# Node rows and kept sums moved in quarters, and VectorE's side tasks dealt anew over eight batches

## The chip, the core and the metric

The kernel runs on one core of one Trainium2 chip. The core has TensorE (PE in the profile), VectorE (DVE), ScalarE (ACT), GpSimd (POOL) and SyncE (SP), which each follow their own instruction stream and wait for one another by semaphores. SP and POOL issue the transfers: SP plain copies between HBM and the on-chip memory SBUF, POOL the gathers (indirect transfers that read rows by a list of indices). 16 DMA engines carry them. TensorE writes to PSUM, eight banks of 2 KB in each of 128 partitions.

The metric is the device time of one execution in microseconds.

## The reference

A graph network's block (PaiNN) on 1250 nodes of 512 numbers and 40,000 edges, sorted by their target node, and then a layer norm of the sum of input and block:

```python
x_j = x[src]
v_j = x_j[:, :384].reshape(E, 128, 3)
s_j = silu(x_j[:, 384:] @ W1 + b1) @ W3 + b3
rbf = sqrt(2 / R_CUT) * sin(n * pi * r / R_CUT) / r          # n = 1..20
cutoff = 0.5 * (cos(pi * r / R_CUT) + 1.0) * (r < R_CUT)
split = s_j * (rbf * cutoff @ W2 + b2)
s1, s2, s3 = split[:, :128], split[:, 128:256], split[:, 256:]
v_msg = v_j * s1[:, :, None] + s3[:, :, None] * edge_attr1[:, None, :]
x = x + segment_sum(concat([v_msg.reshape(E, 384), s2]), dst)
x_j = x[src]
v = x_j[:, :384].reshape(E, 3, 128) @ U
v_V = v @ V
norm = linalg.norm(v_V.reshape(E, 128, 3), axis=2)
h = silu(concat([norm, x_j[:, 384:]]) @ Wu1 + bu1) @ Wu2 + bu2
v = v * h[:, :128, None]
scal = einsum('ijk,ijk->ij', v, v_V) + h[:, 256:]
x = x + segment_sum(concat([v.reshape(E, 384), scal]), dst)
out = layernorm(x0 + x)
```

## The kernel before, in words

The first half of the block depends on an edge only through its source row and its distance. So a table with one row of 640 numbers (2560 bytes) for each node is written to HBM first (`table1`, about the first 25 us). Then the main loop in `windowed` runs over the 40,000 edges in 80 batches, `t` = 0 to 79. A batch has four tiles of 128 edges (the last four batches have fewer), one from each of four neighbouring chunks of 512 sorted edges; four batches make a group, two groups a block of 128 nodes, so a block's edges are done every eight batches. Block `b` "begins" at batch 8b + 8, when its sums are complete.

One batch does this:

- `gather(t + 4)`: POOL issues four indirect transfers (line 746) that fetch the table rows of a batch four batches ahead, into one of five buffers ("rooms", named `more` and `nodes` in the profile). The first of the four waits for `made`, the last matrix product of the factors of the next batch.
- `edge_factors(t + 1)` (line 882): PE computes from the radial basis the factors `eb` of the next batch, in four PSUM banks that exist once. So it waits until VectorE has read the factors of the present batch, and VectorE's next batch waits for it.
- `messages(t)`: VectorE makes the one-hot rows `hot` (L841), two products of the gathered rows with the factors (L893, which waits for the rows, and L896, the last reader of `eb`), `spread` (L851) and the pair of marks `pair` (L911).
- `add_messages(t - 1)` and `count_links(t - 1)`: PE adds the messages by node and counts the edges by source and target, with one-hot rows that ScalarE makes (L863, L873).

Beside the batches runs the work on finished blocks, which a plan deals to the batches by hand. `at(when, step, rank, fn, ...)` puts a task into one of the lists `first`, `early`, `late` and `dve`; in each batch the loop at line 1550 issues `messages`, `first`, the sums and counts, `early`, the factors, the gather, `late` and `dve`, each list in order of rank. An engine carries out what it is given in this order. VectorE's own tasks stand in `dve`, after L911, where PE is busy with the next factors.

For block `b`, with steps counted from its begin, the tasks that matter here are: `sum_block` (PE sums the block in the single PSUM bank `work`, steps 0 and 1), `fetch_nodes` (SP loads the block's 128 rows of x into `node_x`, 256 KB, step -3), `take_block` (VectorE adds both: L1032 for 384 columns, L1037 for 128, step 1), `turn_nodes` (step 3), `keep_rest` (L1042, step 4: VectorE writes x + x1 into the buffer `h_t`, and SP stores it as `resid`, 256 KB), then the second half's products by node, `scale_row` (L1166, step 8), `dot_row` (L1175, step 9), `end_row` (PE, step 10, list `early`, in a `work` bank: L1144, L1145, L1098), and `part_row`, which splits the row into an upper (ScalarE) and a lower part (VectorE, L1205, step 13).

`work()` gives out one PSUM bank; each call takes it anew, for another purpose. The second segment sum is a product of the matrix of edge counts with these split rows: `begin_out` does parts of it ahead, from batch 32 on, in slots of the plan (`ready` says from which batch a unit may run), and stores ("spills", L1297) each started sum through SP, 256 KB. The rest follows after the loop, with the layer norm.

`make_turns` prepares the arguments of the sine for two groups at a time on VectorE: part 0 multiplies (L769), part 1 rounds (L775), part 2 subtracts (L782, twice), part 3 is ScalarE's sine.

Of the kernel before, what the change touches and what calls it, by code (L numbers as in the profile page):

```python
# [11 lines left out]
F32 = mybir.dt.float32  # L12
# [5 lines left out]
ALU = mybir.AluOpType  # L18
# [3 lines left out]
P = 128  # L22
C = 128
V = 3 * C
R_CUT = 1.4415
N_RBF = 20
EPS = 1e-05
MAGIC = 12582912.0
# [562 lines left out]
def windowed(tc, sh):  # L591
# [63 lines left out]
    with tc.tile_pool(name="msg", bufs=4) as pool, tc.tile_pool(  # L655
# [84 lines left out]
        def gather(t, behind=None):  # L740

            g, i = batches[t]
            rows_t = next(rooms)
            for j in tiles(g, i):
                n = lanes(g, i, j)
                got = nc.gpsimd.indirect_dma_start(  # L746
                    out=rows_t[:n, j, :],
                    out_offset=None,
                    in_=sh.table1,
                    in_offset=bass.IndirectOffsetOnAxis(  # L750
                        ap=sh.src_i[:n, g, i * CPG + j : i * CPG + j + 1], axis=0
                    ),
                )
                if behind is not None and j == 0:
                    tc.add_manual_dep(
                        got.ins, behind.ins.name, sync,
                        reason="so that rows come while PE is ahead of DVE",
                    )
            clear_rest(t, rows_t, nc.gpsimd)
            rows_of[t] = rows_t  # L760


        def make_turns(g, n, part):

            shape = [P, n, EPG, N_RBF]
            args = turn[:, :n].rearrange("p g t n -> p (g t n)")
            if part == 0:
                share = ratio[:, g * EPG : (g + n) * EPG].rearrange("p (g t) -> p g t", t=EPG)
                nc.vector.tensor_mul(  # L769
                    turn[:, :n], share[:, :, :, None].to_broadcast(shape),  # L770
                    halves[-1][:, None, None, :].to_broadcast(shape),
                )
            elif part == 1:
                wholes[g] = rbf.tile([P, 2 * N_RBF * EPG], F32, name="whole")[:, : n * N_RBF * EPG]
                nc.vector.tensor_scalar(  # L775
                    wholes[g], args, MAGIC, MAGIC, op0=ALU.add, op1=ALU.subtract
                )
            elif part == 2:
                whole = wholes.pop(g)
                for k in range(n):  # L780
                    cols = slice(k * N_RBF * EPG, (k + 1) * N_RBF * EPG)
                    nc.vector.tensor_sub(args[:, cols], args[:, cols], whole[:, cols])  # L782
            elif part == 3:
                nc.scalar.activation(args, args, AF.Sin, scale=TWO_PI)

        wholes = {}

        basis = sh.basis
        halves, fading = [sh.half_n], {0: fade[:, :EPG]}
# [231 lines left out]
        node_x = sh.node_x  # L1021

        def fetch_nodes(b):
            if b == NB - 1:
                rows = sh.n_nodes + MARGIN - b * P
                nc.gpsimd.memset(node_x[rows // 32 * 32 :, :], 0.0)
            load_nodes(nc.sync, sh, node_x[:, None, :], b, b + 1, slice(0, width), b)

        def take_block(b):
            blk, xb = blks.pop(b), node_x  # L1030
            x1 = pool.tile([P, width], F32, name="x1", bufs=2)
            nc.vector.tensor_add(  # L1032
                x1[:, :V].rearrange("p (c k) -> p k c", k=3),
                xb[:, :V].rearrange("p (c k) -> p k c", k=3),
                by_component(blk[:, :V]),
            )
            nc.vector.tensor_add(x1[:, V:], xb[:, V:], blk[:, V:])  # L1037
            x1s[b] = x1

        def keep_rest(b):  # L1040
            both = sh.h_t[:, :width]
            nc.vector.tensor_add(both, x1s[b], node_x)  # L1042
            if b == NB - 1:
                rest[b] = both
                return
            nc.sync.dma_start(resid[b * P : (b + 1) * P, :], both)


        upd = {}
# [293 lines left out]
            last_step[g] = t  # L1343


        first, early, late, dve = {}, {}, {}, {}

        def at(when, step, rank, fn, *args):
            when.setdefault(step, []).append((rank, fn, args))
# [26 lines left out]
        for b in range(NB):  # L1376
            begin = last_step[2 * b + 1] + 1
            begins.append(begin)
            if b < NB - 1:
                assert begin == 8 * b + 8  # L1380
                at(late, begin, 1, sum_block, b, 0)
                at(first, begin + 1, 1, sum_block, b, 1)
                links_at = (
                    (dve, 1, 1, take_block), (dve, 4, 3, keep_rest), (early, 3, 6, turn_nodes),
                    (early, 4, 1, times_u), (late, 4, 1, times_uv), (late, 5, 1, lengths),
                    (first, 6, 3, root), (late, 6, 1, hidden), (first, 7, 1, curve),
                    (late, 7, 1, factors), (dve, 8, 1, scale_row),
                    (dve, 9 if begin + 10 < NT else 8, 3, dot_row),
                )
# [12 lines left out]
            if b in by_vector:  # L1402
                for step in (4, 8) if b < NB - 1 else (2, 6):
                    if b < NB - 1 and step == 4:
                        at(first, begin + step + 1, 0, add_parts, b)
                    else:
                        at(dve, begin + step, 4, add_parts, b)
            at(dve, begin - 3, 9, fetch_nodes, b)
            for when, step, rank, fn in links_at:
                at(when, begin + step, rank, fn, b)  # L1410
            when, step, rank = last
            if begin + step < NT:
                ends[b] = end = begin + step
                at(when, end, rank, end_row, b)
                parts = (first, end + 1, 2), (dve, end + 3, 2)
            else:
                ends[b] = end = begin + min(step, 9)
                at(first, end, 1, end_row, b)
                parts = ((dve, end, 9),) * 2 if b < NB - 1 else ((dve, end - 1, 2),)
            if b == NB - 3:  # L1420
                parts = parts[0], (dve, NT - 1, 9)
            if b == NB - 2:
                parts = parts[0], (dve, begins[b] + 10, 5)
            for k, (when, step, rank) in enumerate(parts):
                at(when, step, rank, part_row, b, k)
# [16 lines left out]
        after = 0  # L1442
        free_slots = [(8 * c + step, when) for c in range(4, NB) for step, when in slots]
        for chain, a in units:
            ready = max(ends[a] + 4, last_step[2 * chain[0] + 1] + 4, after)
            while free_slots[0][0] < ready:
                free_slots.pop(0)
            step, when = free_slots.pop(0)
            if a == chain[1]:
                block = (a, chain[2], chain[0], 1)  # L1450
                at(dve, step - 1, 9, cast_counts, nc.scalar.copy, "cast", CASTS, NB - 1, [block])
            at(when, step, 8, begin_out, chain, a)
            after = step + 1 if a == chain[2] - 1 else step
# [93 lines left out]
        for t in range(min(ahead, NT)):  # L1547
            gather(t)
        edge_factors(0)
        for t in range(max(*first, *early, *late, *dve) + 1):  # L1550
            if t < NT:
                messages(t)
            run(first, t)
            if 1 <= t <= NT:
                add_messages(t - 1)
                count_links(t - 1)
            run(early, t)
            if t + 1 < NT:
                made = edge_factors(t + 1)
            if t + ahead < NT:  # L1560
                gather(t + ahead, made if t + ahead < NT - 2 else None)
            run(late, t)
            run(dve, t)
        assert NB == ACCS + 3
# [371 lines left out]
```

## Time and profile before

| | us |
|---|---|
| three runs | 479.78, 477.28, 478.63 |
| median | 478.63 |
| the profiled execution | 479.63 |
| its span, first to last instruction | 477.8 |
| VectorE busy | 421.4 |
| TensorE busy (mean granted clock 0.947) | 406.7 |
| ScalarE busy | 372.1 |
| GpSimd busy | 339.3 |

The profile is of one execution. A row of a timeline has the start, the duration, the engine, the line, the operation, what it writes and reads, and in brackets the engine's idle time just before it and what ended it. A row of a group of instructions has the line, the engine, the operation with its tiles, the count, then the busy time, the mean in ns, and the idle time before. "issue" as the end of an idle time means that nothing in the profile was waited for. Names of tiles are the program's own.

### The profile page before, as it was taken

The page shows a single profiled execution, that of the slowest core. Times are in us where ns is not written, and L with a number is a line of the kernel's source. Part 1 is how long each engine was busy: PE and PEld are TensorE (multiplying, and loading weights), DVE is VectorE, ACT ScalarE, POOL GpSimd, SP SyncE. Part 2 cuts the span into 40 slices and gives each one's busy share as a digit, 9 for nine tenths or more (in the row PEclk, how much of TensorE's full clock was granted, in tenths as well). Part 3 has the DMA queues.
Part 4 walks back from the last instruction along what each step waited for, and adds up shares of the span by engine and source line. Part 5 has one row for each costly group of instructions (what it writes and reads, how often), then busy time and mean ns, then how long its engine had stood idle before and what let it go on. Part 6 is the DMA issues. An engine that isn't in the chain of part 4 may idle for free.

```text
span 477.8 us, 11146 instructions
## 1 busy us (share of the span) xinstructions
PE 406.7 (85%) x4233; PEld 230.0 (48%) x4233; DVE 421.4 (88%) x666; ACT 372.1 (78%) x971; POOL 339.3 (71%) x366
## 2 busy tenths in 40 slices
PE   5847678888887887898899899988999989899993
PEld 3423343454444454455445545644554654455782
DVE  5889999888999998899999899998999898896693
ACT  3556877686989879579898899888999798586573
POOL 7367777777777777777777777777777777763940
PEclk9956989897999999799999999999999999899997
DMA  8898888898889889888998988888898898889123
GB/s 255 307 266 262 263 261 257 257 301 259 255 258 308 259 268 301 256 264 259 306 295 278 319 285 286 292 276 275 292 310 284 284 300 271 248 281 365 42 100 123
DMA packets 39107, 126.96 MB, mean 266 GB/s; under 512 B 6801, under 2 KB 9119, under 8 KB 39043
## 3 DMA queue, kind: packets, MB, share of 16 engines
q0 software_dynamic: 25824, 104.47, 69.5%
q1 hardware_dynamic: 11610, 20.56, 12.4%
q10 hardware_dynamic: 1608, 1.12, 0.8%
q8 instruction: 35, 0.57, 0.5%
q14 instruction: 30, 0.24, 0.1%
HBM read 114.78 MB, written 11.34 MB: 264 GB/s over the span
## 4 chain that ended last, share of the span: by engine, by line
PE 24%; DVE 22%; POOL 20%; DMA 16%; issue 13%; ACT 2%; DVEq 0%; ACTq 0%; POOLq 0%
POOL more L746 14%; DMA more<-table,src_i 10%; POOL nodes L746 6%; DVE more L896 6%; PE eb L882 6%; DMA nodes<-table,src_i 5%; DVE more L893 4%; PE agg L927 3%; DVE nodes L896 3%; DVE spread L851 2%; PE agg L933 2%; PE eb L1279 1%; PE adj L1279 1%; DVE nodes L893 1%; PE pp L311 1%
## 5 line engine op out<-in xcount | busy, mean ns | idle before, releaser
L746 POOL DMA_INDIRECT more<-table,src_i x189 | 182.7, 967 | 66.1 <-issue 48.3
L746 POOL DMA_INDIRECT nodes<-table,src_i x124 | 119.1, 960 | 37.8 <-issue 31.7
L873 ACT ACTIVATE one<-one,weight,src_f 128x128 f16<-128x128 f16 x313 | 128.5, 482 | 0.4 <-DVE src_f L723 0.2
L882 PE MATMUL eb<-w_sb,basis_t 25*128 25x388 f32 x626 | 79.2, 564 | 48.8 <-DVE more L896 29.8
L863 ACT ACTIVATE one<-number,low 128x128 f16<-128x128 f16 x313 | 99.7, 392 | 2.4 <-PE adj L956 2.4
L896 DVE TENSOR_TENSOR more<-more,eb 128x1536 f32<-128x1536 f32 (+2 forms) x49 | 82.8, 1691 | 0.0
L893 DVE TENSOR_TENSOR more<-more,eb 128x1024 f32<-128x1024 f32 (+2 forms) x49 | 57.7, 1178 | 8.2 <-issue 4.7
L882 PEld LDWEIGHTS eb<-w_sb,basis_t 25*128 25x128 f32 x626 | 26.5, 193 | 70.0 <-DVE more L896 41.8
L896 DVE TENSOR_TENSOR nodes<-nodes,eb 128x1536 f32<-128x1536 f32 (+1 forms) x32 | 54.3, 1697 | 0.0
L927 PE MATMUL agg<-more,hot 128*32 128x512 f32 x378 | 54.0, 636 | 0.0
L933 PEld LDWEIGHTS agg<-more,spread 128*32 128x32 f32 x1134 | 35.6, 116 | 31.1 <-issue 31.0
L851 DVE TENSOR_TENSOR spread<-hot,eb 128x384 f32<-128x384 f32 (+1 forms) x81 | 43.2, 534 | 0.0
L893 DVE TENSOR_TENSOR nodes<-nodes,eb 128x1024 f32<-128x1024 f32 (+1 forms) x32 | 37.9, 1183 | 5.8 <-DMA nodes<-table,src_i 5.2
L933 PE MATMUL agg<-more,spread 128*32 128x128 f32 x1134 | 42.9, 285 | 0.0
L911 DVE TENSOR_TENSOR pair<-number,column 128x640 f16<-128x640 f16 (+1 forms) x81 | 38.7, 479 | 0.0
L841 DVE TENSOR_TENSOR hot<-lane,eb 128x128 f32<-128x128 f32 (+1 forms) x81 | 22.6, 280 | 16.8 <-PE eb L882 16.6
L956 PE MATMUL adj<-pair,one 128*128 128x160 f16 x313 | 36.8, 241 | 0.0
L927 PE MATMUL agg<-nodes,hot 128*32 128x512 f32 x248 | 35.6, 630 | 0.0
L933 PEld LDWEIGHTS agg<-nodes,spread 128*32 128x32 f32 x744 | 22.8, 113 | 20.5 <-issue 20.4
L956 PEld LDWEIGHTS <-one 128*128 128x128 f16 x313 | 22.3, 102 | 13.1 <-issue 11.8
L933 PE MATMUL agg<-nodes,spread 128*32 128x128 f32 x744 | 27.5, 277 | 0.0
L824 ACT COPY basis_t<-work 128x512 f32<-128x512 f32 x20 | 11.7, 586 | 19.3 <-PE work L819 19.2
(268 smaller groups left out, 679.9 us busy)
## 6 DMA issues: line engine op xcount, KB each, us to landing
table<-more SPq DMA_DIRECT2D x10, 320.0 KB
spilled<-begun SPq DMA_DIRECT2D x12, 256.0 KB
more<-table,src_i POOLq DMA_INDIRECT x189
more<-spilled SPq DMA_DIRECT2D x2, 1280.0 KB
resid<-h_t SPq DMA_DIRECT2D x9, 256.0 KB
node_x<-in_x_dram SPq DMA_DIRECT2D x8, 256.0 KB
nodes<-table,src_i POOLq DMA_INDIRECT x124
nodes<-in_x_dram POOLq DMA_DIRECT2D x2, 768.0 KB
```

The lines of the kernel that those rows point to most:

```text
L746: got = nc.gpsimd.indirect_dma_start(out=rows_t[:n, j, :], out_offset=None, in_=sh.table1, in_offset=bass.IndirectOffsetOnAxis(ap=sh.src_i ...
L841: nc.vector.tensor_tensor(hots[t][:m, js, :], lane[:m, None, :WIN].to_broadcast(shape), eb[:m, js, V + 3 : V + 4].to_broadcast(shape), op= ...
L851: nc.vector.tensor_mul(spread[t][:m, js], hots[t][:m, js, None, :].to_broadcast(shape), eb[:m, js, V : V + 3, None].to_broadcast(shape),)
L863: nc.scalar.activation(onehots[t][:, j, :], number[:, :P], AF.Abs, bias=low[:, e : e + 1])
L873: nc.scalar.activation(one, one, AF.Relu, scale=less[:, e : e + 1], bias=worth[:, e : e + 1])
L882: made = nc.tensor.matmul(eb[:, j, : V + CARRY], turned[g][rows, i, :], sh.w2_sb[rows, :], start=True, stop=True,)
L893: nc.vector.tensor_mul(msg[:m, js, V:], msg[:m, js, V:], eb[:m, js, C:V])
L896: nc.vector.tensor_mul(msg[:m, js, :V].rearrange("p t (k c) -> p t k c", k=3), msg[:m, js, :V].rearrange("p t (k c) -> p t k c", k=3), eb[ ...
L911: nc.vector.tensor_tensor(pair[:m, js, :].rearrange("p t (l h) -> p t l h", h=2), number[:m, : PARTS * WIN].rearrange("p (l h) -> p l h", ...
L927: nc.tensor.matmul(agg[j * WIN : (j + 1) * WIN, :], hots[t][:, j, :], msg[:, j, :width], start=(i == 0), stop=False, skip_group_check=True,)
L933: nc.tensor.matmul(agg[j * WIN : (j + 1) * WIN, c * C : (c + 1) * C], spread[t][:, j, c, :], msg[:, j, width:], start=False, stop=(i == la ...
L956: nc.tensor.matmul(to[:, :, at : at + WIN], one[:m, j, :], pair[:m, j, :].rearrange("e (p n) -> e p n", n=WIN), start=(i == 0 and j == js[ ...
```

## The change

- `fetch_nodes` of blocks 0 to 8 becomes `fetch_part` in four batches, steps -3 to 0: 32 of 128 rows each, 64 KB. The store of `resid` leaves `keep_rest` and becomes `keep_part` in four batches, steps 8 to 11, for blocks 0 to 7. Both stand in a new list `mid`, which is issued after the gather and before `late`, and each transfer waits for `made`, PE's factors of the next batch. Blocks 8 and 9 keep whole transfers for what is left.
- `take_block` is split: `take_v` (L1032) stays at step 1, `take_s` (L1037) goes to step 2.
- The lower half of `part_row` (L1205) goes from step 13 to step 11. With it `ready` in the plan of the second sum goes from ends + 4 to ends + 2.
- Parts 1 and 2 of `make_turns` no longer round both groups and then subtract for both, but do both for one group each, with a rounding of 320 numbers instead of 640.

```diff
-            elif part == 1:
-                wholes[g] = rbf.tile([P, 2 * N_RBF * EPG], F32, name="whole")[:, : n * N_RBF * EPG]
-                nc.vector.tensor_scalar(
-                    wholes[g], args, MAGIC, MAGIC, op0=ALU.add, op1=ALU.subtract
-                )
-            elif part == 2:
-                whole = wholes.pop(g)
-                for k in range(n):
+            elif part in (1, 2):
+                for k in range(part - 1, min(part, n)):
                     cols = slice(k * N_RBF * EPG, (k + 1) * N_RBF * EPG)
-                    nc.vector.tensor_sub(args[:, cols], args[:, cols], whole[:, cols])
+                    whole = rbf.tile([P, N_RBF * EPG], F32, name="whole", bufs=2)
+                    nc.vector.tensor_scalar(
+                        whole, args[:, cols], MAGIC, MAGIC, op0=ALU.add, op1=ALU.subtract
+                    )
+                    nc.vector.tensor_sub(args[:, cols], args[:, cols], whole)
...
+        QUARTER = P // 4
+
+        def fetch_part(b, k):
+            low, high, node = places(sh, b)
+            first, end = max(low, k * QUARTER), min(high, (k + 1) * QUARTER)
+            at_node = node + first - low
+            for i, j in by_sixteen(end - first):
+                after_factors(nc.sync.dma_start(
+                    node_x[first + i : first + j, :], sh.x[at_node + i : at_node + j, :]
+                ))
+
+        def after_factors(got):
+            tc.add_manual_dep(
+                got.ins, made.ins.name, sync, reason="so that transfers spread over the batches"
+            )
+
+        def keep_part(b, k):
+            rows = slice(k * QUARTER, (k + 1) * QUARTER)
+            after_factors(nc.sync.dma_start(
+                resid[b * P + rows.start : b * P + rows.stop, :], sh.h_t[rows, :width]
+            ))
...
+        def take_s(b):
+            nc.vector.tensor_add(x1s[b][:, V:], node_x[:, V:], blks.pop(b)[:, V:])
...
             if b == NB - 1:
                 rest[b] = both
-                return
-            nc.sync.dma_start(resid[b * P : (b + 1) * P, :], both)
+            if b == NB - 2:
+                nc.sync.dma_start(resid[b * P : (b + 1) * P, :], both)
...
-                    (dve, 1, 1, take_block), (dve, 4, 3, keep_rest), (early, 3, 6, turn_nodes),
+                    (dve, 1, 1, take_v), (dve, 2, 1, take_s), (dve, 4, 3, keep_rest),
+                    (early, 3, 6, turn_nodes),
...
-            at(dve, begin - 3, 9, fetch_nodes, b)
+            if b < NB - 1:
+                for k in range(4):
+                    at(mid, begin - 3 + k, 1, fetch_part, b, k)
+            else:
+                at(dve, begin - 3, 9, fetch_nodes, b)
+            if b < NB - 2:
+                for k in range(4):
+                    at(mid, begin + 8 + k, 2, keep_part, b, k)
...
-                parts = (first, end + 1, 2), (dve, end + 3, 2)
+                parts = (first, end + 1, 2), (dve, end + 1, 6)
...
-            ready = max(ends[a] + 4, last_step[2 * chain[0] + 1] + 4, after)
+            ready = max(ends[a] + 2, last_step[2 * chain[0] + 1] + 4, after)
...
                 gather(t + ahead, made if t + ahead < NT - 2 else None)
+            run(mid, t)
             run(late, t)
             run(dve, t)
```

More of the change, by code (lines that the diff above doesn't have):

```diff
@@ L772, in make_turns @@
                 )
-            elif part == 1:
-                wholes[g] = rbf.tile([P, 2 * N_RBF * EPG], F32, name="whole")[:, : n * N_RBF * EPG]
-                nc.vector.tensor_scalar(
-                    wholes[g], args, MAGIC, MAGIC, op0=ALU.add, op1=ALU.subtract
-                )
-            elif part == 2:
-                whole = wholes.pop(g)
-                for k in range(n):
-                    cols = slice(k * N_RBF * EPG, (k + 1) * N_RBF * EPG)
-                    nc.vector.tensor_sub(args[:, cols], args[:, cols], whole[:, cols])
+            elif part in (1, 2):
+                for k in range(part - 1, min(part, n)):
+                    cols = slice(k * N_RBF * EPG, (k + 1) * N_RBF * EPG)
+                    whole = rbf.tile([P, N_RBF * EPG], F32, name="whole", bufs=2)
[3 more added lines that the diff above has]
+                    nc.vector.tensor_sub(args[:, cols], args[:, cols], whole)
             elif part == 3:
                 nc.scalar.activation(args, args, AF.Sin, scale=TWO_PI)
-        wholes = {}
         basis = sh.basis
@@ L1023, in fetch_nodes, with take_v @@
         def fetch_nodes(b):
-            if b == NB - 1:
-                rows = sh.n_nodes + MARGIN - b * P
-                nc.gpsimd.memset(node_x[rows // 32 * 32 :, :], 0.0)
+            rows = sh.n_nodes + MARGIN - b * P
+            nc.gpsimd.memset(node_x[rows // 32 * 32 :, :], 0.0)
             load_nodes(nc.sync, sh, node_x[:, None, :], b, b + 1, slice(0, width), b)
-        def take_block(b):
-            blk, xb = blks.pop(b), node_x
-            x1 = pool.tile([P, width], F32, name="x1", bufs=2)
+        QUARTER = P // 4
[16 more added lines that the diff above has]
+            ))
+        def take_block(b):
+            take_v(b)
+            take_s(b)
+        def take_v(b):
+            blk, xb = blks[b], node_x
+            x1s[b] = x1 = pool.tile([P, width], F32, name="x1", bufs=2)
             nc.vector.tensor_add(
@@ L1036, in take_block @@
             )
-            nc.vector.tensor_add(x1[:, V:], xb[:, V:], blk[:, V:])
-            x1s[b] = x1
+        def take_s(b):
+            nc.vector.tensor_add(x1s[b][:, V:], node_x[:, V:], blks.pop(b)[:, V:])
         def keep_rest(b):
@@ L1343, in windowed @@
             last_step[g] = t
-        first, early, late, dve = {}, {}, {}, {}
+        first, early, late, dve, mid = {}, {}, {}, {}, {}
         def at(when, step, rank, fn, *args):
@@ L1549, in windowed @@
         edge_factors(0)
-        for t in range(max(*first, *early, *late, *dve) + 1):
+        for t in range(max(*first, *early, *late, *dve, *mid) + 1):
             if t < NT:
```

## The prediction

> **What bounds the kernel now.** I read the page first: VectorE (DVE) is the busiest engine by its share, TensorE (PE) next, GpSimd (POOL) only fourth.
>
> ```profile
> span 477.8 us, 11146 instructions
> PE 406.7 (85%) x4233; PEld 230.0 (48%) x4233; DVE 421.4 (88%) x666; ACT 372.1 (78%) x971; POOL 339.3 (71%) x366
> ...
> L746 POOL DMA_INDIRECT more<-table,src_i x189 | 182.7, 967 | 66.1 <-issue 48.3
> L746 POOL DMA_INDIRECT nodes<-table,src_i x124 | 119.1, 960 | 37.8 <-issue 31.7
> ...
> L893 DVE TENSOR_TENSOR more<-more,eb 128x1024 f32<-128x1024 f32 (+2 forms) x49 | 57.7, 1178 | 8.2 <-issue 4.7
> ...
> L893 DVE TENSOR_TENSOR nodes<-nodes,eb 128x1024 f32<-128x1024 f32 (+1 forms) x32 | 37.9, 1183 | 5.8 <-DMA nodes<-table,src_i 5.2
> ```
>
> The share misleads. The 313 gathers of GpSimd have idle time between them that waits for nothing ("issue"). Their own line, and their timeline, show why:
>
> ```profile
> L746 POOL DMA_INDIRECT more<-table,src_i x189: 914/946/1402, 25.7 to 417.2; - x189
> L746 POOL DMA_INDIRECT nodes<-table,src_i x124: 942/946/1266, 41.0 to 422.2; - x124
> ```
>
> ```profile
> 75.04 0.95 POOL L746 DMA_INDIRECT nodes<-table,src_i  x1 [0.30 <-DMA nodes<-table,src_i]
> ...
> 77.54 1.14 POOL L746 DMA_INDIRECT more<-table,src_i  x1 [0.30 <-issue]
> 78.98 0.94 POOL L746 DMA_INDIRECT more<-table,src_i  x1 [0.30 <-issue]
> 80.23 0.95 POOL L746 DMA_INDIRECT more<-table,src_i  x1 [0.30 <-issue]
> ...
> 82.73 1.11 POOL L746 DMA_INDIRECT more<-table,src_i  x1 [0.30 <-DVE nodes L896]
> ```
>
> A gather takes 0.95 us and the next starts 0.30 later: 1.25 us each (78.98 to 80.23), four to a batch, 5.00 us a batch. From the first start, 25.7, to the last, 422.2, 312 such steps would be 390.0 us; they took 396.5. So GpSimd issues without a pause for the whole loop, and all that it ever loses is 6.5 us of lengthened gathers. VectorE's own pace is in the starts of L841, which opens a batch (batches 32 to 40):
>
> ```profile
> 199.84 0.29 DVE L841 TENSOR_TENSOR hot<-lane,eb 128x128 f32<-128x128 f32 x1 [1.15 <-PE eb L882]
> ...
> 204.57 0.28 DVE L841 TENSOR_TENSOR hot<-lane,eb 128x128 f32<-128x128 f32 x1
> ...
> 209.03 0.28 DVE L1037 TENSOR_TENSOR x<-node_x,work 128x128 f32<-128x128 f32 x1
> 209.23 0.56 DVE L1175 TENSOR_TENSOR square<-x,vv 128x384 f32<-128x384 f32 x1
> 209.69 0.29 DVE L841 TENSOR_TENSOR hot<-lane,eb 128x128 f32<-128x128 f32 x1
> ...
> 213.15 0.49 DVE L911 TENSOR_TENSOR pair<-number,column 128x640 f16<-128x640 f16 x1
> 213.55 0.49 DVE L807 TENSOR_TENSOR basis<-turn,adj 128x320 f32<-128x320 f32 x1
> 214.45 0.29 DVE L841 TENSOR_TENSOR hot<-lane,eb 128x128 f32<-128x128 f32 x1 [0.41 <-PE eb L882]
> ...
> 219.05 0.29 DVE L841 TENSOR_TENSOR hot<-lane,eb 128x128 f32<-128x128 f32 x1 [0.26 <-PE eb L882]
> ...
> 223.92 0.28 DVE L841 TENSOR_TENSOR hot<-lane,eb 128x128 f32<-128x128 f32 x1
> ...
> 227.78 0.68 DVE L1205 TENSOR_TENSOR lower<-x,upper 128x512 fp32r<-128x512 f32 x1
> 228.38 0.81 DVE L769 TENSOR_TENSOR turn<-ratio,adj 128x640 f32<-128x640 f32 x1
> 229.11 0.28 DVE L841 TENSOR_TENSOR hot<-lane,eb 128x128 f32<-128x128 f32 x1
> ...
> 233.71 0.29 DVE L841 TENSOR_TENSOR hot<-lane,eb 128x128 f32<-128x128 f32 x1 [0.25 <-PE eb L882]
> ...
> 238.38 0.28 DVE L841 TENSOR_TENSOR hot<-lane,eb 128x128 f32<-128x128 f32 x1
> ```
>
> The eight batches take 4.73, 5.12, 4.76, 4.60, 4.87, 5.19, 4.60 and 4.67: 38.5 us against GpSimd's 40.0. VectorE is 1.5 us quicker in each eight, catches up, and then waits for rows; L893's waits (8.2 + 5.8 = 14 us) are that. A VectorE stall costs the end nothing unless it is among the last.
>
> **What lengthens a gather.** While VectorE has caught up (from batch 8):
>
> ```profile
> 77.38 0.48 DVE L911 TENSOR_TENSOR pair<-number,column 128x640 f16<-128x640 f16 x1
> ...
> 79.27 1.22 DVE L893 TENSOR_TENSOR nodes<-nodes,eb 128x1024 f32<-128x1024 f32 x1 [0.47 <-DMA nodes<-table,src_i]
> ...
> 82.54 0.48 DVE L911 TENSOR_TENSOR pair<-number,column 128x640 f16<-128x640 f16 x1
> ...
> 84.49 1.22 DVE L893 TENSOR_TENSOR more<-more,eb 128x1024 f32<-128x1024 f32 x1 [0.50 <-DMA more<-table,src_i]
> ```
>
> The gather at 77.54 starts inside L911 (77.38 to 77.86) and takes 1.14 instead of 0.95; that at 82.73 starts inside L911 (82.54 to 83.02) and takes 1.11. Both gain the rest of L911 less 0.13 us: 0.32 - 0.13 = 0.19, 0.29 - 0.13 = 0.16. [...] This phase is locked: rows of a batch land 3.3 us after the end of its last gather (75.99 to 79.27, 81.18 to 84.49), L911 starts 3.27 after that (79.27 to 82.54), 6.55 in all; the sixth gather from there starts 0.30 + 5 x 1.25 = 6.55 later, plus the 0.16 just lost. So at the floor of the lag (3.3 us) every batch pays about 0.18.
>
> [...]
>
> **The change, part by part.**
>
> Nodes and sums in pieces. Two transfers of 256 KB per eight batches, issued one behind the other, become eight of 64 KB, each issued behind PE's factors of a batch. Bytes are the same. The burst does delay rows today:
>
> ```profile
> 180.84 0.33 SPq L1046 DMA_DIRECT2D resid<-h_t  x1
> 181.26 0.38 SPq L417 DMA_DIRECT2D node_x<-in_x_dram  x1
> ```
>
> ```profile
> 188.79 1.22 DVE L893 TENSOR_TENSOR more<-more,eb 128x1024 f32<-128x1024 f32 x1 [2.19 <-issue]
> ```
>
> 2.19 us of VectorE's time go there, but GpSimd goes on, so the end gains 0; what the stall did do was to push VectorE's lag off the floor where L911 meets a gather. SP's eight issues cost it 8 x 0.38 = 3 us in 40. SP now waits for PE before each piece; behind it stand only the spills (L1297). The last node piece leaves as batch 8b+9 opens and take_v reads it a batch of work later (209.69 to 213.55, 3.9 us). No row shows such a piece alone; the nearest is a gather's last transfer, 3.3 us from GpSimd's end to L893 (above). So it lands 0.6 us early, or, were it as slow as the rows of batch 73 (some 5 us, below), 1.1 us late. I take it on time, by the nearer row. A late one makes VectorE's lag longer, which GpSimd does not feel. The same holds for the last kept piece, which keep_rest must wait for before it writes that buffer again. What stands behind the pieces at GpSimd is nothing: the gathers keep their place and their own wait for the factors, which they have never waited on for long (0.30 before each row above).
>
> VectorE's tasks. L1037 (0.20, 209.03 to 209.23) leaves the 5.12 batch, L1205 (0.60, 227.78 to 228.38) the 5.19 one for a 4.60 one; each half of the rounding (half of 0.48, plus one subtraction of 0.4) stands in its own batch, under the 0.81 that the 4.67 batch holds today. New: 4.73, 4.92, 4.60, 4.86, 4.87, 4.60, 4.60, 4.60 = 37.8. The 0.7 us gained per eight is again worth 0 at GpSimd's pace; it brings the floor sooner.
>
> A new wait. take_s now reads the block's sum in the one "work" bank in batch 8b+10 (dve list), but end_row of the block before takes that bank earlier in the same batch (early list). The bank can be handed over only after its last reader, so PE stops there, with the factors of the next batch behind it and VectorE behind those; on ScalarE (ACT) the copy of end_row's result waits too, with the carry of the basis and the next one-hot rows behind it, which PE needs only a batch later. Today:
>
> ```profile
> 211.99 0.22 PE L1144 MATMUL work<-bias,ones_r 65*128 65x128 bf16 x1
> ...
> 213.45 0.94 PE L882 MATMUL eb<-w_sb,basis_t 25*128 25x388 f32 x8
> ```
>
> L1144 to the factors: 1.46; factors to L841: 1.00 (213.45 to 214.45). take_s would end at 213.55 + 0.28 = 213.83, so L841 comes at 213.83 + 1.46 + 1.00 = 216.3, not 214.45: that batch takes 6.6. The eight then take 39.8, still under 40.0. It comes eight times (batches 18, 26 ... 74). If the bank were handed over without that wait, the batch would stay at 4.60 and the lag at its floor for longer; the two ends of this wait are thus 0 and 2.0 us a time at VectorE, and I take the upper one because one bank serves both tiles. It lifts the lag by 6.6 - 5.0 = 1.6, and seven batches at a mean of 4.74 bring it back at about 0.3 to 0.45 each: floor again after four or five.
>
> The sum. Batches 6 to 17, no such wait and no burst: floor, 12 x 0.18 = 2.2. Of the 56 from 18 to 73, half at the floor, 28 x 0.18 = 5.0, half at today's mean of 6.5 / 79 = 0.08, 2.3. The other twelve at 0.08: 1.0. Together 10.5 against 6.5: +4.0. Ends of this term: -6.5 (none) and 74 x 0.18 - 6.5 = +6.8 (all); I stay between, by the rows at 77.54 and 82.73. The end:
>
> ```profile
> 406.83 1.22 DVE L893 TENSOR_TENSOR nodes<-nodes,eb 128x1024 f32<-128x1024 f32 x1 [1.95 <-DMA nodes<-table,src_i]
> ...
> 411.74 0.28 DVE L841 TENSOR_TENSOR hot<-lane,eb 128x128 f32<-128x128 f32 x1
> ...
> 417.71 0.29 DVE L841 TENSOR_TENSOR hot<-lane,eb 128x128 f32<-128x128 f32 x1 [1.63 <-PE eb L882]
> ```
>
> Batch 73's last gather, the 296th, ends near 25.7 + 296 x 1.25 + some 6 (the part of the 6.5 lost so far) = 401.7, so its rows take some 5 us instead of 3.3. After it no gather is waited for any more, and VectorE and PE set the time: what GpSimd loses before, 4.0 us more, moves everything after it, and what is won or lost here counts in full. L1037 leaves that batch, -0.2. Batch 74 gets the bank wait, but PE is 1.63 late there already: 6.6 against 417.71 - 411.74 = 6.0, +0.5 with the end of that lateness. Total +4.3. The profiled execution took 479.6, one above the median of the runs, 478.6; on the median: **482.9 us**.
>
> **Rivals.** *Faster.* The 1.95 and 1.63 at the end go with the smoother traffic: 478.6 - 3.6 = 475.0. It decides if rows of batch 73 land at 3.3 us. Against it: the spill of 256 KB issued ahead of it keeps its place: with `ready` at ends + 2 the planner moves only units of batches 36 to 49, none after 50. *No change.* Lag off the floor (pieces delay rows by 0.2 to 0.4), L911 misses the gathers as in most of today's run: 478.6 + 0.3 = 478.9. *Bank wait as the bound.* VectorE's 39.8 leaves 0.2 per eight; one stall of 2.2 (row 188.79) in each of the seven eights from batch 18 makes 42.0 against GpSimd's 40.8 (40.0 + 0.1 a batch): 7 x 1.2 = 8.4, 487.0. Against it: the bursts go.
>
> **Chances.** Forecast 0.45, bank wait as the bound 0.12, no change 0.24, faster 0.19. Slower by over 0.5% is the first two, 0.57 (0.5%, 2.4 us, is about what a measurement here can tell from no change). Range 475.5 to 488: from the faster rival to the bank wait as the bound plus a microsecond; the forecast's own is 480 to 486.
>
> **What would show it.** Right: gathers back to back from 26 to some 427; their mean over 0.975 us; many of 1.1 to 1.2 starting inside L911, L893 waiting briefly in most batches; L1144 waiting for take_s's addition and L841 starting 6.6 us later in batches 18, 26 and so on. Wrong: gathers as short as before, or GpSimd waiting for something; or the waits of 1.95 and 1.63 gone from the end.

## The result, and the profile after

| | before | after |
|---|---|---|
| median, us | 478.23 (four runs beside the changed kernel) | 492.0 |
| runs, us | 477.28 to 479.78 | 488.58, 491.1, 492.9, 495.33 |
| ratio of after to before, 95% interval | | 1.0263 [1.0221, 1.0305] |
| the profiled execution, us | 479.63 | 488.58 (the quickest of the four) |
| its span, us | 477.8 | 486.8 |

The change makes the kernel 2.6% slower. The direction was forecast, the size (482.9, up to 488.0) was not. The page of the changed kernel (line numbers have moved: L841 is now L837, L882 L878, L893 L889, L896 L892, L911 L907, L1144 L1166; take_v is L1053, take_s L1060):

```profile
span 486.8 us, 11283 instructions
PE 408.7 (84%) x4233; PEld 231.0 (47%) x4233; DVE 423.6 (87%) x675; ACT 372.3 (76%) x971; POOL 339.0 (70%) x366
...
L746 POOL DMA_INDIRECT more<-table,src_i x189 | 181.5, 960 | 68.1 <-issue 47.1
L746 POOL DMA_INDIRECT nodes<-table,src_i x124 | 120.1, 968 | 44.2 <-issue 32.6
...
L889 DVE TENSOR_TENSOR more<-more,eb 128x1024 f32<-128x1024 f32 (+2 forms) x49 | 57.6, 1176 | 1.5 <-DMA more<-table,src_i 1.2
...
L837 DVE TENSOR_TENSOR hot<-lane,eb 128x128 f32<-128x128 f32 (+1 forms) x81 | 22.4, 278 | 28.6 <-PE eb L878 28.4
```

All engines are as busy as before within 2.2 us; the 9 us are waiting. The gathers are not longer: 181.5 + 120.1 = 301.6 us busy against 182.7 + 119.1 = 301.8. And VectorE no longer waits for rows, 1.5 us at L889 (all of it in the group shown) in place of 14: it has become the late one. What it waits for is PE's factors: 28.4 us at L837, where the kernel before has

```profile
DVE hot L841 <- PE eb L882: 16.6, 37, 1.6
```

The view of waits after the change says what PE waits for:

```profile
DVE hot L837 <- PE eb L878: 28.4, 21, 3.4
ACT x L1218 <- PE work L1120: 28.1, 8, 5.8
...
PE work L1166 <- DVE x L1060: 19.6, 8, 5.8
```

Eight times PE stands at L1166 (end_row) for take_s, 19.6 us in all: seven waits of 1.6 to 2.5 us, and one of 5.8. One of the seven, in batch 66, first on PE and then on VectorE:

```profile
381.94 0.45 PE L952 MATMUL adj<-pair,one 128*128 128x160 f16 x4
384.34 0.23 PE L1166 MATMUL work<-bias,ones_r 65*128 65x128 bf16 x1 [1.96 <-DVE x L1060]
...
385.81 0.93 PE L878 MATMUL eb<-w_sb,basis_t 25*128 25x388 f32 x8
```

```profile
380.15 0.27 DVE L837 TENSOR_TENSOR hot<-lane,eb 128x128 f32<-128x128 f32 x1
...
383.61 0.48 DVE L907 TENSOR_TENSOR pair<-number,column 128x640 f16<-128x640 f16 x1
384.01 0.28 DVE L1060 TENSOR_TENSOR x<-node_x,work 128x128 f32<-128x128 f32 x1
...
386.81 0.29 DVE L837 TENSOR_TENSOR hot<-lane,eb 128x128 f32<-128x128 f32 x1 [2.13 <-PE eb L878]
```

take_s stands on VectorE behind the whole batch's products; PE cannot take the bank before 384.34, sends the next factors at 385.81, and VectorE idles 2.13 us until they are there. The batch takes 386.81 - 380.15 = 6.66 us, as the forecast said (6.6). Four of the eight batches are like it (6.66 or 6.67); the other four take 7.5 to 8.0. Where GpSimd loses its time is in the timeline of its gathers:

```profile
303.88 0.94 POOL L746 DMA_INDIRECT nodes<-table,src_i  x1 [3.44 <-PE eb L878]
...
310.21 0.94 POOL L746 DMA_INDIRECT more<-table,src_i  x1 [1.64 <-PE eb L878]
...
346.64 0.94 POOL L746 DMA_INDIRECT more<-table,src_i  x1 [0.89 <-DMA more<-table,src_i]
...
430.29 0.94 POOL L746 DMA_INDIRECT nodes<-table,src_i  x1 [3.59 <-PE agg L929]
431.54 0.95 POOL L746 DMA_INDIRECT nodes<-table,src_i  x1 [0.30 <-DVE hot L827]
```

Back to back until 300 us, then four waits in place of 0.30: 3.14 + 1.34 + 0.59 + 3.29 = 8.4 us. With a start 1.3 us later (27.0 for 25.7) and 0.2 less in the gathers that is 9.5; the last gather starts at 431.54 in place of 422.2, 9.3 later. The whole loss of the profiled execution is in these waits: VectorE and PE fall behind bit by bit, and GpSimd may issue only four batches ahead of them.

The first two of the four waits stand right behind a second wait of VectorE, which comes from the quarters and not from the split. In batch 49, just before a bank wait, take_v is late:

```profile
289.99 0.34 SPq L1319 DMA_DIRECT2D spilled<-begun  x1
290.42 0.38 SPq L1031 DMA_DIRECT2D node_x<-in_x_dram  x1
```

```profile
294.62 0.68 DVE L1053 TENSOR_TENSOR x<-node_x,work 128x384 f32<-128x384 f32 x1 [3.17 <-PE adj L952]
```

The last quarter of the block's node rows leaves only at 290.42, behind a spill on SP's queue, though batch 49 had opened at 287.51. The profile names L952, whose result take_v does not read; that the wait is for this quarter is inferred from the order. In the next batch PE's wait for take_s is then the one of 5.8 us, and that batch takes 8.0.

### The profile page after: what moved, and what is told of

Its sections match the earlier page's. It is cut to its first block, busy times and chain, and to the rows that moved or that the text cites. A ratio compares the mean times of both kernels' runs of the same rounds, so it can differ in the third digit from the quotient of the medians.

```text
span 486.8 us, 11283 instructions
## 1 busy us (share of the span) xinstructions
PE 408.7 (84%) x4233; PEld 231.0 (47%) x4233; DVE 423.6 (87%) x675; ACT 372.3 (76%) x971; POOL 339.0 (70%) x366
## 4 chain that ended last, share of the span: by engine, by line
DVE 39%; PE 26%; DMA 11%; issue 10%; POOL 7%; ACT 5%; DVEq 0%; SPq 0%; POOLq 0%
DVE more L892 9%; DVE more L889 6%; PE eb L878 6%; POOL more L746 5%; DVE nodes L892 5%; DVE spread L847 4%; DMA more<-table,src_i 4%; DVE pair L907 3%; DVE nodes L889 3%; PE agg L923 3%; DMA nodes<-table,src_i 3%; PE work L1120 2%; POOL nodes L746 2%; DMA dst_r<-in_dst_dram 2%; PE agg L929 2%
## 5 line engine op out<-in xcount | busy, mean ns | idle before, releaser
L746 POOL DMA_INDIRECT more<-table,src_i x189 | 181.5, 960 | 68.1 <-issue 47.1
L746 POOL DMA_INDIRECT nodes<-table,src_i x124 | 120.1, 968 | 44.2 <-issue 32.6
L878 PE MATMUL eb<-w_sb,basis_t 25*128 25x388 f32 x626 | 79.8, 568 | 36.1 <-DVE more L892 24.8
L892 DVE TENSOR_TENSOR more<-more,eb 128x1536 f32<-128x1536 f32 (+2 forms) x49 | 82.7, 1690 | 0.0
L889 DVE TENSOR_TENSOR more<-more,eb 128x1024 f32<-128x1024 f32 (+2 forms) x49 | 57.6, 1176 | 1.5 <-DMA more<-table,src_i 1.2
L892 DVE TENSOR_TENSOR nodes<-nodes,eb 128x1536 f32<-128x1536 f32 (+1 forms) x32 | 54.3, 1696 | 0.0
L878 PEld LDWEIGHTS eb<-w_sb,basis_t 25*128 25x128 f32 x626 | 26.6, 193 | 56.5 <-DVE more L892 36.0
L929 PEld LDWEIGHTS agg<-more,spread 128*32 128x32 f32 x1134 | 35.4, 116 | 31.8 <-issue 31.6
L837 DVE TENSOR_TENSOR hot<-lane,eb 128x128 f32<-128x128 f32 (+1 forms) x81 | 22.4, 278 | 28.6 <-PE eb L878 28.4
L929 PE MATMUL agg<-more,spread 128*32 128x128 f32 x1134 | 42.7, 284 | 0.0
L907 DVE TENSOR_TENSOR pair<-number,column 128x640 f16<-128x640 f16 (+1 forms) x81 | 38.6, 477 | 0.0
L889 DVE TENSOR_TENSOR nodes<-nodes,eb 128x1024 f32<-128x1024 f32 (+1 forms) x32 | 37.8, 1180 | 0.0
L952 PE MATMUL adj<-pair,one 128*128 128x160 f16 x313 | 36.2, 238 | 0.0
L923 PE MATMUL agg<-nodes,hot 128*32 128x512 f32 x248 | 34.1, 605 | 0.0
L929 PEld LDWEIGHTS agg<-nodes,spread 128*32 128x32 f32 x744 | 22.2, 110 | 19.2 <-issue 19.2
L952 PEld LDWEIGHTS <-one 128*128 128x128 f16 x313 | 22.0, 101 | 12.8 <-issue 10.9
L929 PE MATMUL agg<-nodes,spread 128*32 128x128 f32 x744 | 26.8, 273 | 0.0
L820 ACT COPY basis_t<-work 128x512 f32<-128x512 f32 x20 | 11.7, 586 | 19.6 <-PE work L815 19.6
```

What stands on the lines that cost most here:

```text
L746: got = nc.gpsimd.indirect_dma_start(out=rows_t[:n, j, :], out_offset=None, in_=sh.table1, in_offset=bass.IndirectOffsetOnAxis(ap=sh.src_i ...
L837: nc.vector.tensor_tensor(hots[t][:m, js, :], lane[:m, None, :WIN].to_broadcast(shape), eb[:m, js, V + 3 : V + 4].to_broadcast(shape), op= ...
L878: made = nc.tensor.matmul(eb[:, j, : V + CARRY], turned[g][rows, i, :], sh.w2_sb[rows, :], start=True, stop=True,)
L889: nc.vector.tensor_mul(msg[:m, js, V:], msg[:m, js, V:], eb[:m, js, C:V])
L892: nc.vector.tensor_mul(msg[:m, js, :V].rearrange("p t (k c) -> p t k c", k=3), msg[:m, js, :V].rearrange("p t (k c) -> p t k c", k=3), eb[ ...
L907: nc.vector.tensor_tensor(pair[:m, js, :].rearrange("p t (l h) -> p t l h", h=2), number[:m, : PARTS * WIN].rearrange("p (l h) -> p l h", ...
```

## The experiments

Two theories stood against each other. *Bank wait*: the split of take_block alone costs, because end_row now waits for take_s; VectorE's and PE's loop becomes the bound. *The rest of the change*: pieces, the new deal, or lengthened gathers cost. The runs fell on several chips. On two of them the kernel before takes 588 to 589 us, with a bound of its own (last section), so each edit has two columns; ratios to the kernel before on the same chip, with 95% intervals. Where an expectation is in microseconds, it can be held only against the right column.

| edit | where before takes 588 to 589 | where before takes 479 to 481 |
|---|---|---|
| the change | 1.0167 [1.0124, 1.021] | 1.0263 [1.0221, 1.0305] |
| the change, take_s back at step 1 | 1.0019 [0.9983, 1.0054], 1.0022 [0.9987, 1.0057] | 0.9961 [0.993, 0.9992] |
| before, split alone | 1.0088 [1.0057, 1.012], 1.0044 [0.9999, 1.0089] | 1.0201 [1.014, 1.0261] |
| the change, end_row later | 1.0052 [1.0022, 1.0082] | 1.0108 [1.0061, 1.0155] |
| before, every other split | | 1.0026 [1.0003, 1.0049] |
| before, pieces alone | 1.0084 [1.0051, 1.0116] | 0.9985 [0.996, 1.001] |
| before, tasks alone | 1.001 [0.9975, 1.0045] | 1.0015 [0.9993, 1.0037] |

(The change itself in the right column is the result above, with 478.23 for the kernel before.)

**take_s back beside take_v**, everything else as changed:

```diff
-                    (dve, 1, 1, take_v), (dve, 2, 1, take_s), (dve, 4, 3, keep_rest),
+                    (dve, 1, 1, take_v), (dve, 1, 1, take_s), (dve, 4, 3, keep_rest),
```

> The changed kernel with take_s back at step 1, so that both reads of the block's sum end before end_row takes the work bank. If the wait for that bank is what costs (19.6 us of TensorE waiting for L1060 in eight places): 476 to 481 us, no wait of TensorE for take_s, batches 18, 26 and so on at 4.6 us instead of 6.7 to 7.6. If the pieces and their waits for the factors cost: 487 or more. If the lengthened gathers at the floor of the lag cost, as was forecast: 481 to 484, with the gathers' excess over 0.95 us at 9 us or more in all (5.6 in the changed kernel, 6.4 before).

> The changed kernel with take_s back at the step of take_v, so that end_row no longer stands between the bank's writer and take_s; pieces and all other tasks as changed. Theory 'bank wait as the bound': 0.993 to 1.005 of the kernel before (475 to 481 where that is 478), VectorE's first operation of batches 18, 26, ... 74 no longer waits 2.1 us or more for PE, and no gather waits. Theory 'pieces or lengthened gathers': 1.015 or more, with those waits gone all the same.

> The changed kernel with take_s back at the step of take_v. Theory 'bank wait as the bound': 0.993 to 1.005 of the kernel before on either kind of chip (1.002 twice where the kernel before takes 588). Theory 'pieces or lengthened gathers': 1.015 or more where the kernel before takes 478.

One list entry takes back the whole loss: 1.0263 becomes 0.9961, at 479.11 us. Its view of waits, where the kernel before takes 481:

```profile
DVE hot L837 <- PE eb L878: 9.2, 22, 1.1
...
DVE more L889 <- DMA more<-table,src_i: 6.5, 11, 1.5
...
DVE nodes L889 <- DMA nodes<-table,src_i: 4.1, 4, 2.4
```

VectorE waits for rows again (10.6 us), as before the change. The interval ends 0.1% under the kernel before, less than the half per cent that can be told apart; the other chips gave 1.002 twice. It is the version to keep, not one that is shown to be faster.

**The split alone**, in the kernel before:

```diff
-                    (dve, 1, 1, take_block), (dve, 4, 3, keep_rest), (early, 3, 6, turn_nodes),
+                    (dve, 1, 1, take_v), (dve, 2, 1, take_s), (dve, 4, 3, keep_rest),
+                    (early, 3, 6, turn_nodes),
```

> The kernel before with take_block split over steps 1 and 2 and nothing else. If the bank wait is the cause: 487 to 495 us by itself, with TensorE waiting some 2 us for take_s in eight batches. If the cause lies in the pieces or in the moved tasks: 476 to 480.

> The kernel before with its addition of the kept block split over two steps, and nothing else: no pieces, tasks as before. Theory 'bank wait as the bound': the eight stalls of 2.1 to 3.4 us come back, and where the kernel before takes 478 the time is 1.010 to 1.027 of it (483 to 491). Theory 'the rest of the change': 0.997 to 1.005 (477 to 480).

> The kernel before with the addition of the kept block split over two steps, alone. Theory 'bank wait as the bound': 1.010 to 1.027 of the kernel before where that takes 478, less where it takes 588 (1.009 and 1.004 measured), since there PE is late by itself. Theory 'the rest of the change': 0.997 to 1.005.

2.0% slower, with neither pieces nor the new deal. Its waits (L1149 is end_row here, L1043 take_s):

```profile
DVE hot L841 <- PE eb L882: 34.7, 36, 3.1
...
PE work L1149 <- DVE x L1043: 15.2, 8, 2.2
...
POOL nodes L746 <- PE agg L933: 6.6, 1, 6.6
```

The same eight waits, and GpSimd waits too: once for 6.6 us, and six times for PE's factors, 6.0 us in all.

**end_row later**, behind the next batch's factors, the split kept:

```diff
-                last = (early, 10, 6)
+                last = (late, 10, 0)
```

> The changed kernel with end_row moved behind the next batch's factors, so that the bank is still the writer's when take_s reads it in the second step: the split stays, only what takes the bank between goes. Theory 'bank wait': 0.993 to 1.007 of the kernel before, no wait of PE for take_s over 1 us. Theory 'the split costs by itself, or the pieces do': 1.015 or more.

> The changed kernel with end_row behind the next batch's factors, the split kept. Theory 'bank wait': 0.993 to 1.007 of the kernel before (1.005 measured where that takes 588). Theory 'the split costs by itself, or the pieces do': 1.015 or more where it takes 478.

A miss of the bank theory's numbers: 1.0108 where at most 1.007 was expected. PE's wait for take_s is gone, but the split is not free. The view of waits, then ScalarE and VectorE in batch 35:

```profile
ACT x L1218 <- PE work L1120: 30.6, 8, 7.6
...
PEld L1166 <- DVE x L1060: 3.9, 7, 0.6
```

```profile
215.99 0.27 ACT L1218 COPY x<-work 128x128 f32<-128x128 f32 x1 [3.19 <-PE work L1120]
```

```profile
214.56 0.29 DVE L837 TENSOR_TENSOR hot<-lane,eb 128x128 f32<-128x128 f32 x1
...
219.04 0.49 DVE L803 TENSOR_TENSOR basis<-turn,adj 128x320 f32<-128x320 f32 x1 [0.53 <-PE adj L952]
...
220.37 0.29 DVE L837 TENSOR_TENSOR hot<-lane,eb 128x128 f32<-128x128 f32 x1 [0.24 <-PE eb L878]
```

ScalarE's copy of end_row's result comes later now, its queue stands behind that copy (30.6 us in eight waits, against 8.9 in five in the kernel before), and the next batch takes 220.37 - 214.56 = 5.81. So the split lengthens a batch in this order too, by ScalarE and not by PE's wait for take_s; reading the bank in the batch before end_row's, as the kernel before does, avoids both. That this makes the 1.08% is not shown: in the profiled execution, the quickest of seven (482.61), no gather waits over 0.4 us.

**Every other block.** Does each wait cost its share, or nothing until VectorE's slack is used up?

```diff
-                    (dve, 1, 1, take_v), (dve, 2, 1, take_s), (dve, 4, 3, keep_rest),
+                    (dve, 1, 1, take_v), (dve, 1 + b % 2, 1, take_s), (dve, 4, 3, keep_rest),
```

> The kernel before with take_s a step later for every other block of nodes (1, 3, 5 and 7) and the sum in one step for the rest: four waits of 2 to 3 us, sixteen batches apart, in place of eight. Theory 'threshold' (VectorE has some 2 us per eight batches in hand, and only what goes beyond shows): two eights of 39.8 to 42 and 38.5 stay near 80, so 0.997 to 1.006 of the kernel before, no gather waits over 0.3 us. Theory 'each wait costs alike': half of the 2.0 % that eight cost, 1.008 to 1.012, where the kernel before takes 478 to 481; where it takes 588 the two can't be told apart (0.998 to 1.006 by both).

The split alone, for blocks 1, 3, 5 and 7. Its waits:

```profile
PE work L1149 <- DVE x L1043: 7.3, 4, 2.2
```

Half the waits are there (7.3 us of PE in place of 15.2), and they cost 0.26%, not half of 2.0%: the interval ends at 1.0049, below the 1.008 expected if each wait cost alike. No gather of the loop waits over 0.4 us. VectorE's waits for rows between batches 18 and 74 fall from 10.3 us to 1.2, so the four waits used up nearly all that it had in hand. The threshold it is.

**The pieces alone, the new deal alone**, each in the kernel before, with the diff's own lines (the kept sums in quarters and the rounding in halves belong to them, as the change has them):

```diff
+            if b < NB - 1:
+                for k in range(4):
+                    at(mid, begin - 3 + k, 1, fetch_part, b, k)
+            else:
+                at(dve, begin - 3, 9, fetch_nodes, b)
```

```diff
-                parts = (first, end + 1, 2), (dve, end + 3, 2)
+                parts = (first, end + 1, 2), (dve, end + 1, 6)
...
-            ready = max(ends[a] + 4, last_step[2 * chain[0] + 1] + 4, after)
+            ready = max(ends[a] + 2, last_step[2 * chain[0] + 1] + 4, after)
```

> The kernel before with the nodes and kept sums in pieces alone. By the bank wait as the cause: 475 to 481, the waits of 1 to 2 us for rows in batches 14, 30, 46 gone, the end unmoved since GpSimd sets the pace. If pieces of 64 KB behind the factors come late: VectorE waits at take_block or keep_rest, 484 or more.

> The kernel before with node rows and kept sums moved in quarters, and nothing else. Theory 'the split alone costs': 0.996 to 1.004 where the kernel before takes 478 to 481 (1.008 where it takes 588). Theory 'the pieces cost too, and the new deal of the tasks pays it back': 1.006 to 1.012 on both.

> The kernel before with the lower part at step 11, ready at ends + 2 and the rounding in halves, no pieces, no split. By the bank wait as the cause: 475 to 481, batch of step 13 0.6 us shorter, the end unmoved. If the moved spills or tasks are a cause: 482 or more.

> The kernel before with the tasks of angles and rounding dealt as in the changed kernel, and nothing else. Theory 'VectorE's spread is worth nothing while GpSimd sets the pace': 0.996 to 1.004 (1.001 where the kernel before takes 588). Theory 'the new deal pays back what the pieces cost': 0.988 to 0.994 where the kernel before takes 478 to 481.

Both are worth nothing where the gathers set the pace (0.9985 and 1.0015). Where they do not, the pieces cost 0.8% in the one comparison made; with the new deal beside them (take_s back) nothing was left of it. Why they cost there was not followed. The pieces are not always on time, all the same. With the pieces alone, where the gathers set the pace:

```profile
DVE x L1053 <- DMA node_x<-in_x_dram: 5.4, 4, 3.4
```

In each of the four profiles with pieces on these chips, take_v waits once for 3.2 to 3.8 us. Without the split this cost nothing (0.9985, and 0.9961 with take_s back).

**The two kernels themselves**, for comparison on the chips:

> The changed kernel itself, so that the three beside it are compared on one chip. On a chip where the kernel before takes about 478, both theories: 1.022 to 1.031 of the kernel before (488 to 493). On a chip where the kernel before takes about 588 (PE's instruction issue is the bound there): theory 'bank wait' expects 1.010 to 1.020, since the split alone gave 1.009 and the pieces alone 1.008 there.

> The kernel before itself, for its profile beside the others on the same chip. Where it takes about 588: PE stands still for about 110 us in sum with nothing that the profile names ahead of it (54 us in the profile of 478), GpSimd waits for PE's factors in most batches, and a batch takes about 6.1 us; then the gathers do not set the pace there, with or without the change. Where it takes about 478: as profiled before, 4.9 us a batch.

The change costs 1.7% where the kernel before takes 589, of which putting take_s back returns 1.45%. The kernel before, run once by itself, came to a chip of the other kind: 479.75, and its gathers were back to back. What was expected of it where it takes 588 was not measured.

## Why the prediction was right and wrong

**GpSimd as the bound: right for the kernel before.** So the pieces (0) and the new deal (0) were right too, as the two runs alone show. But a quarter was not on time, as the forecast took it, nor 1.1 us late at worst: take_v waited 3.2 for it in batch 49, and with the bank waits on top GpSimd did feel it.

**Lengthened gathers, +4.0: wrong.** Their busy time went from 301.8 to 301.6. The step that failed is the half of 56 batches at the floor of the lag. In the changed kernel VectorE did not wait for rows once from batch 18 to batch 74, so the lag never came back to its floor there. With take_s back, where no bank wait lifts the lag, it waited for rows some 15 times (11 + 4) in 80 batches, not in most, so the phase in which L907 meets a gather of each batch does not last.

**The new wait: the mechanism right, the size wrong.** Place, cause and number came as worked out: eight waits, four of them with a batch of 6.66 or 6.67. What failed is the sentence "The eight then take 39.8, still under 40.0", and both of its terms were too small. It adds 2.0 to 37.8, and 37.8 comes from one eight (batches 32 to 40, 38.5 us), which was among the quickest, less 0.7 for the new deal. What VectorE needs on average stands in its first operations of batches 18 and 74 (the latter, 411.74, is quoted in the prediction) and its waits between them, in the kernel before:

```profile
127.70 0.27 DVE L841 TENSOR_TENSOR hot<-lane,eb 128x128 f32<-128x128 f32 x1
```

```profile
DVE more L893 <- issue: 4.7, 5, 2.2
DVE nodes L893 <- DMA nodes<-table,src_i: 2.7, 2, 2.0
DVE more L893 <- DMA more<-table,src_i: 2.3, 3, 1.4
...
DVE nodes L893 <- issue: 0.6, 1, 0.6
```

Seven eights took 411.74 - 127.70 = 284.0 us, 40.6 each, and 10.3 us of them were waits for rows. So VectorE's slack was 1.5 us an eight: it needs 39.1. With the new deal alone the same working gives (286.1 - 13.7) / 7 = 38.9, not 37.8. And the bank wait adds more than 2.0: batches 18, 26 and so on to 66 took 7.25 us on average, against 4.64 before, 2.6 more. 39.1 and 2.6 make 41.7, over the gathers' 40.6, and the late quarter adds 3.2 once, 0.5 an eight. In the changed kernel:

```profile
126.37 0.28 DVE L837 TENSOR_TENSOR hot<-lane,eb 128x128 f32<-128x128 f32 x1
...
420.69 0.28 DVE L837 TENSOR_TENSOR hot<-lane,eb 128x128 f32<-128x128 f32 x1
```

294.3 us, 42.0 an eight, and no wait for rows among them. Waits every sixteen batches lengthened an eight by 1.4 on average, within the slack, and were nearly free.

The end (+0.5, and -0.2 for L1037) was of no weight: from the last gather to the end it took 55.3 us, before 55.6, and GpSimd's four waits carried 8.4. Two of the forecast's signs of being wrong came: gathers as short as before, and GpSimd waiting.

The rival "bank wait as the bound", given 0.12, named the right bound. That its 8.4 us is so near the measured 9.0 of span is in part luck: it came to 42.0 an eight by adding a stall of 2.2 behind a burst of transfers to 39.8, and no such stall was left. The medians lie 13.8 apart, since the other runs of the changed kernel are up to 6.8 us slower than the profiled one. No profile shows where; their granted clock is lower (0.943, 0.939, 0.932 and 0.927 for 488.58, 491.1, 492.9 and 495.33), which fits the last section but does not prove it.

## What to carry to other kernels

When an engine is said to have slack, take it from what it waited for over the whole loop (waits divided by rounds), not from the quickest round: the one gave 1.5 us, the other 2.2, and the added wait was 2.1 to 3.4. A read of a single buffer that moves behind another engine's next use of it turns into a wait of that engine, and then of all behind it (here eight waits of PE, 19.6 us, and eight of VectorE behind them, 21.0); look at who takes the buffer next before moving its last reader. Here waits below the slack were nearly free (four of them, 1.0026), and those above it cost what exceeded it, late in the loop (eight, 1.0201), so a test with half the waits tells a threshold from a price for each wait.

## What the runs showed of the hardware

**Behind three of the seven waits of 1.6 to 2.5 us TensorE's granted clock was 0.50.** In the profile of the changed kernel the granted clock is 0.50 in stretches of 3.41 us, or of multiples of that, and the stretches start whole multiples of it apart (131.19, 172.15 and 254.07: 12 and 24). Windows laid on this grid, the one in which a bank wait lies and the one after it (columns: window, length, PE busy, PEld, DVE, ACT, POOL, granted clock, DMA share, GB/s), for batches 18 and 42, then 26 and 34:

```profile
127.78:131.19 3.41, 0.87 (x9) 0.67 (x7) 3.13 (x6) 0.04 (x1) 2.80 (x3) 1.00 0.89 290
131.19:134.60 3.41, 3.41 (x18) 2.04 (x16) 0.63 (x2) 0.42 (x2) 2.50 (x4) 0.50 0.85 260
250.66:254.07 3.41, 1.83 (x31) 1.44 (x20) 2.77 (x5) 0.70 (x2) 2.50 (x4) 1.00 0.90 298
254.07:257.48 3.41, 3.41 (x15) 1.80 (x14) 1.08 (x2) 0.42 (x2) 2.76 (x3) 0.50 0.86 269
```

```profile
168.74:172.15 3.41, 1.06 (x13) 0.85 (x10) 3.16 (x6) 0.93 (x3) 2.77 (x3) 1.00 0.89 299
172.15:175.56 3.41, 3.41 (x18) 2.08 (x16) 0.59 (x2) 0.42 (x2) 2.52 (x3) 0.50 0.83 257
209.69:213.11 3.42, 1.85 (x37) 1.45 (x30) 3.09 (x5) 1.25 (x4) 2.74 (x3) 1.00 0.89 296
213.11:216.52 3.41, 3.41 (x38) 1.85 (x40) 1.61 (x3) 1.48 (x5) 2.56 (x3) 1.00 0.83 262
```

After a window in which PE was busy 0.87, 1.83 or 1.06 us (its waits were 2.5, 1.6 and 2.4) the clock is 0.50 in the next; after 1.85 (a wait of 1.6) it is 1.00. PE's busy time alone does not draw the line: a window of the same profile from 421.32, with 1.70 busy, is followed by 1.00. What does was not shown. VectorE waited 2.1 us at L837 behind the four waits with the clock at 1.00, and 3.0 to 3.1 behind the three with 0.50, so the price that the forecast had put on a wait was too low for half of the eight batches (the longest, 3.4, is that of batch 50). Whether this explains the spread of the kernel's runs was not shown.

**A gather that starts inside L907 is still longer**, so the term was rightly seen and wrongly counted:

```profile
247.40 0.48 DVE L907 TENSOR_TENSOR pair<-number,column 128x640 f16<-128x640 f16 x1
```

```profile
247.51 1.18 POOL L746 DMA_INDIRECT nodes<-table,src_i  x1 [0.30 <-issue]
```

1.18 against the 0.94 of the gathers above: rest of L907 0.37, less 0.13, is 0.24, the rule of the prediction. It holds for the 17 gathers of this profile that start with 0.20 to 0.41 us of L907 left, which took 1.02 to 1.23, and for those with 0.10 to 0.15 left, 0.95 to 0.97. It does not hold for the four that start right with L907, 0.52 or 0.53 us before its end: they took 0.94 or 0.95.

**Chips differ.** Where the kernel before takes 588 to 589, instructions of VectorE take about as long as elsewhere (with take_s back 0.67 us each on average, 118.02 us for 175 of them between 200 and 360 us, against 0.69, 266.44 us for 385 between 125.9 and 413.6, on the chip of 479), but PE stands idle for nothing that the profile names. The change with take_s back, on such a chip:

```profile
PEld eb L878 <- issue: 69.8, 58, 5.4
PEld agg L929 <- issue: 64.6, 156, 2.7
...
POOL more L746 <- PE eb L878: 39.4, 20, 4.5
```

Up to 5.4 us at a time ahead of the factors, so GpSimd waits for PE there, and the gathers are not the bound. In the same kernel on the chip of 479 the "issue" waits of L878 come to less than 1 us, and the longest of L929 is 0.7. That PE's instructions come late there, as the expectation for the change itself has it, was the author's reading of these waits; no run tested it.
